# Half-width expert group: tokens as the stationary operand, weights as the moving one, and later weight splits for the next group

## The chip, the cores and the metric

The kernel runs on one core of one Trainium2 chip. The metric is the device time of one execution in microseconds; where several runs were made, their median stands. The profile is one execution of its own, taken by the hardware profiler; a granted TensorE clock of 1.00 means that nothing was throttled.

## What is computed

The reference has two parts. The first is a set of small two-layer networks over x of shape 128 batches x 64 tokens x 256:

```python
s0 = relu(x @ swi[0]) @ swo[0]            # shared, all batches
s1 = relu(x @ swi[1]) @ swo[1]
eo = relu(x @ wi[label]) @ wo[label]      # expert of the batch, 5 experts
w  = softmax(relu(concat(eo[:,0], s0[:,0], s1[:,0]) @ g1) @ g2)
x  = x + eo * w[:,0] + s0 * w[:,1] + s1 * w[:,2]
```

The inner width F is 1024. The second part is one diffusion step with reflected edges on the result, each batch with its own factors. The change concerns only the line `eo`.

## The kernel before

Every fp32 operand of the large products is split into a high part (rounded by a copy on ScalarE) and a low part (the remainder, a subtraction on VectorE or GpSimd), both of type float32r (`split`, L121). A product is then three matmuls: high by high, and the two mixed ones.

A table built on the chip sorts the 128 batches by expert into slots. After the two shared networks' first token tile and five large expert tiles, the remaining slots run as nine groups (`GROUPS`, L31 to L33), in this order: groups 0 to 2 of 8 batches (512 token columns), group 3 of 2 batches (128 columns, "the half", `HALF`), group 4 of 8 batches, groups 5 to 8 of 4 batches (256 columns). Each group is one expert, so it needs its own weights: 4 loads of 512 KB (`load_group_w`, L439), each with two blocks of F of 128, and in each block 256 columns of W-in and 256 of W-out.

A group's work, for each of the eight blocks f of F:

- `split_group_w` (L466) splits the block's 512 weight columns: one copy on ScalarE, one subtraction on VectorE.
- `up` (L918) computes h for this block: six matmuls, with a 128x128 piece of W-in as the stationary operand and the group's token columns as the moving one. h comes out with F on the partitions and tokens in the columns, which is what the next product needs. ScalarE takes the relu as h's high part, VectorE the low part.
- `down` (L932) takes two blocks at a time: 128 tokens of h are the stationary operand, W-out the moving one. Per 128 tokens and block there is a wide matmul (high h by high and low W-out, 512 columns) and a narrow one (low h by high W-out, 256 columns). After the last block `store_group` (L957) adds the two halves of the accumulator (a ScalarE copy, a VectorE addition) and sends them to the table `eo_d` in DRAM.

`stream` (L1011) sets the order. A step is two blocks of F (`LAG`); in each it calls, for both, `ahead` and `up`, and then `down` of the step before. `ahead` (L965) holds everything done in advance: loads of the next or next but one group, the split of its tokens (`split_group_x`, L458; the low part on GpSimd), and one split of the next group's weights per block. Around the half the pattern is bent: during the half only four of group 4's eight splits are made, the other four during group 4's first four blocks, along with those of group 5:

```python
if g == HALF + 1 and f + 4 < NF:
    split_group_w(g, f + 4)
if g + 1 < NRUN:
    if f == (0 if g == HALF else 4):
        split_group_x(g + 1)
    if g != HALF or f < 4:
        split_group_w(g + 1, f)
```

Matmuls and SP's DMA issues are always marked to stay in program order (`mm`, L91; `dma`, L118). VectorE's, ScalarE's and GpSimd's instructions are marked so only while `in_order(True)` holds (L115); in `stream` that is during the half. Elsewhere a scheduler places them. Each of these engines then executes its own queue strictly in the order built, and the same holds for SP, which issues the loads.

Buffers come from pools: 25 tiles of 4 KB per partition for weights, 16 of 2 KB for h and results, and eight PSUM banks, of which six are `psum` and two `seeded`. A tile waits for the last user of the tile that had the buffer before.

Of the kernel before, what the change touches and what calls it, by code (L numbers as in the profile page):

```python
# [8 lines left out]
F32 = mybir.dt.float32  # L9
F32R = mybir.dt.float32r  # L10
I32 = mybir.dt.int32
AF = mybir.ActivationFunctionType
# [4 lines left out]
P = 128  # L17
B, S, D, F = 128, 64, 256, 1024
NE = 5
NF = F // P  # L20
# [8 lines left out]
HALF = NBIG - 1  # L29
# [10 lines left out]
LAG = 2  # L40
# [9 lines left out]
def cond_resid_kernel(ctx: ExitStack, tc: tile.TileContext, xg, xs, xn, itok, z, we, ws, g1, g2, out):  # L50
# [11 lines left out]
    nc = tc.nc  # L62
# [6 lines left out]
    ppool = ctx.enter_context(tc.tile_pool(name="ppool", bufs=6, space=bass.MemoryType.PSUM))  # L69
# [8 lines left out]
    def psum(name):  # L78
        return ppool.tile([P, 512], F32, tag="ps", name=name)
# [5 lines left out]
    def slot4(name, dtype=F32R):  # L85
        return pool4.tile([P, 2, 512], dtype, tag="t4", name=name)

    def slot2(name, dtype=F32):
        return small.tile([P, 512], dtype, tag="s2", name=name)

    def mm(out_ap, lhsT, rhs, start, stop):  # L91
        tc.keep_in_program_order(
            nc.tensor.matmul(out_ap, lhsT=lhsT, rhs=rhs, start=start, stop=stop, skip_group_check=True)  # L93
        )
# [18 lines left out]
    vec, act, gps = (Ordered(engine) for engine in (nc.vector, nc.scalar, nc.gpsimd))  # L113

    def in_order(on):  # L115
        Ordered.on = on

    def dma(dst, src):  # L118
        tc.keep_in_program_order(nc.sync.dma_start(dst, src))

    def split(dst_hi, dst_lo, src, lo_eng):  # L121
        act.activation(dst_hi, src, AF.Copy)
        lo_eng.tensor_tensor(dst_lo, src, dst_hi.bitcast(F32), ALU.subtract)
# [27 lines left out]
    def load_wo(u):  # L151
        wop[u] = slotw(f"wo{u}", [P, 2, 2, D], F32R)
        dma(flat_wo(u), wo_d[u])
# [28 lines left out]
    def load_wi(n, q):  # L182
        u = (n % 2) * NQ + q
        w = win.tile([P, 2, 7, P], F32R, tag="w", name=f"wi{n}_{q}")
        dma(w.bitcast(F32), wi_d[u])
        wip[n * NQ + q] = w
# [4 lines left out]
    def load_x(p, order=((0, 0), (1, 0), (0, 1), (1, 1))):  # L191
        for k, l in order:
            xraw[p, k, l] = slot2(f"xr{p}_{k}{l}")
            dma(xraw[p, k, l], xs[2 * p + l, :, k, :])
# [61 lines left out]
    ident = const.tile([P, P], F32, name="ident")  # L256
# [125 lines left out]
    graw, gw, gxr, gx, gval = {}, {}, {}, {}, {}  # L382
# [3 lines left out]
    def own(g, key, make):  # L386

        if g < NRUN:
            return make()
        if key not in spare:  # L390
            spare[key] = make()
        return spare[key]
# [15 lines left out]
    def load_group_x(g):  # L408
        s0, n = GROUPS[g]
        xr = gxr[g] = group_tile(g, [P, n, 2 * S], F32, "gxr")  # L410
        load_batches(s0, n, lambda j: xr[:, j, :])
# [8 lines left out]
    def group_expert(g):  # L420
        gval[g] = expert_of(GROUPS[g][0])
# [17 lines left out]
    def load_group_w(g):  # L439
        group_expert(g)  # L440
        for h in range(NQ):
            r = own(g, ("raw", h), lambda: slot4(f"gwr{g}_{h}", F32))
            dma(r, we[bass.ds(gval[g], 1), :, 2 * h : 2 * h + 2, :].rearrange("o p f c -> p (o f) c"))
            graw[g, 2 * h], graw[g, 2 * h + 1] = r[:, 0, :], r[:, 1, :]

    def load_group(g):
# [19 lines left out]
    def split_group_w(g, f):  # L466
        w = own(g, ("w", f), lambda: slot4(f"gw{g}_{f}"))
        split(w[:, 0, :], w[:, 1, :], graw[g, f], vec)
        gw[g, f] = w


    eot, yb, sh = {}, {}, {}
# [168 lines left out]
    def run(work):  # L641
        for w in work:
            w()
# [272 lines left out]
    hbuf, gacc, total = {}, {}, []  # L916

    def up(g, f):  # L918
        w, (xh, xl), cols = gw[g, f], gx[g], GROUPS[g][1] * S
        ps = own(g, ("up", f % 2), lambda: (seeded if f % 2 and cols == 512 else psum)(f"up{g}_{f}"))  # L920
        todo = [(k, wp, xx) for k in range(2) for wp, xx in ((0, xh), (0, xl), (1, xh))]
        for i, (k, wp, xx) in enumerate(todo):
            mm(ps[:, :cols], w[:, wp, k * P : (k + 1) * P], xx[:, k, :], i == 0, i == len(todo) - 1)
        hi = own(g, ("h", f), lambda: slot2(f"gh{g}_{f}", F32R))
        lo = slot2(f"gl{g}_{f}", F32R) if cols == 512 else hi[:, 256:512]
        act.activation(hi[:, :cols], ps[:, :cols], AF.Relu)
        vec.scalar_tensor_tensor(
            lo[:, :cols], ps[:, :cols], 0.0, hi[:, :cols].bitcast(F32), ALU.max, ALU.subtract
        )
        hbuf[g, f] = hi, lo  # L930

    def down(g, fs):  # L932

        w = [gw.pop((g, f)) for f in fs]
        m = GROUPS[g][1] * S // P
        h = [hbuf.pop((g, f)) for f in fs]
        if fs[0] == 0:
            gacc[g] = [
                own(g, ("acc", i), lambda: ppool.tile([P, 2, D], F32, tag="ps", name=f"gacc{g}_{i}")) for i in range(m)
            ]  # L940

        def wide(i):
            for j, f in enumerate(fs):
                mm(gacc[g][i], h[j][0][:, i * P : (i + 1) * P], w[j][:, :, 256:512], f == 0, False)

        def narrow(i):
            for j, f in enumerate(fs):
                mm(gacc[g][i][:, 0, :], h[j][1][:, i * P : (i + 1) * P], w[j][:, 0, 256:512], False, f == NF - 1)
            if fs[-1] == NF - 1:
                store_group(g, i)  # L950

        work = [lambda i=i, part=part: part(i) for part in (wide, narrow) for i in range(m)]
        if (g, fs[-1]) == (NRUN - 1, NF - 1):
            return work
        run(work)

    def store_group(g, i):  # L957
        acc = gacc[g][i]
        o = own(g, ("o", i), lambda: small.tile([P, D], F32, tag="s2", name=f"ge{g}_{i}"))
        act.activation(o, acc[:, 0, :], AF.Copy)  # L960
        vec.tensor_add(o, acc[:, 1, :], o)
        r0 = GROUPS[g][0] * S + i * P
        dma(eo_d.rearrange("r (s d) -> (r s) d", d=D)[r0 : r0 + P, :], o)

    def ahead(g, f):  # L965

        if g >= NRUN:
            return
        if f == 0:
            if g == NRUN - 3:  # L970
                slots = nc.values_load(
                    tab[0:1, NSLOT + NU : NSLOT + NU + 1], min_val=0, max_val=NSLOT,
                    skip_runtime_bounds_check_because="the table's entries are bounded on the chip",
                )
                total.append(slots)
            if g + 1 < NRUN:
                if g <= NBIG and g != HALF:
                    load_group_w(g + 1)
                if g != HALF:
                    load_group_x(g + 1)  # L980
            if g < 2:
                reload(g)
            for u in range(3 * g, min(3 * g + 3, 2 * NQ)):
                load_wo(u)
            if g == NRUN - 2:
                load_x(1)
            if g == NRUN - 1:
                load_wi(2, 0)
                load_wi(2, 1)
                load_row()  # L990
        if f == 5 and g < 2:
            again(g)
        if g + 1 == HALF and f == 4:
            load_group_x(g + 2)
        if f == 6 and (g + 1 == HALF or NBIG <= g < NRUN - 2):
            load_group_w(g + 2)
        if g == 0 and f + FIRST < NF:
            split_group_w(0, f + FIRST)
        if g == HALF + 1 and f + 4 < NF:
            split_group_w(g, f + 4)  # L1000
        if g + 1 < NRUN:
            if f == (0 if g == HALF else 4):
                split_group_x(g + 1)
            if g != HALF or f < 4:
                split_group_w(g + 1, f)
        elif f < 7:
            if f < 4:
                sum_x(1, T1 + f, gps)
            split_x(1, (B11, B21, T2, T3, T1, T4, B22)[f], vec)

    def stream(g0, g1):  # L1011
        steps = [(g, tuple(range(f, f + LAG))) for g in range(g0, g1) for f in range(0, NF, LAG)]
        for i in range(len(steps) + 1):
            if i < len(steps):
                in_order(steps[i][0] == HALF)
                for f in steps[i][1]:
                    ahead(steps[i][0], f)
                    up(steps[i][0], f)
            if i >= 1:
                rest = down(*steps[i - 1])  # L1020
        return rest


# [49 lines left out]
    def reload(u):  # L1073
        e, q = divmod(u, NQ)
        load_raw(u, ws[e, :, 2 * q : 2 * q + 2, :])
# [43 lines left out]
    for n in range(EI, EI + NQUAD):  # L1119
        parts = [weights_of(n)]  # L1120
# [14 lines left out]
    rest = stream(0, NRUN)  # L1135
# [61 lines left out]
    for p in range(1, NP):  # L1197
        ta, tb = 2 * p, 2 * p + 1
        for e in range(2):
            n = 2 * p + e  # L1200
            parts = [ahead_w(n)]
# [86 lines left out]
```

## Time and profile before

| | us |
|---|---|
| three runs, median (lowest, highest) | 1038.5 (1038.21, 1038.73) |
| the profiled execution, whole | 1038.9 |
| its span | 1037.1 |
| DMA, mean over the span | 153 GB/s |
| chain that ended last, TensorE's share | 57% |
| groups: first up matmul, last down matmul | 299.1, 444.4 |

The page counts busy time as the time in which an engine has at least one instruction under way. PE is the matmul, PEld the weight load for it, which overlaps matmuls; DVE is VectorE, ACT ScalarE, POOL GpSimd, SP the engine that issues the DMAs. Matmul records overlap each other, so the distance from one start to the next is the cost of one, not the record's length. In the groups of instructions, these rows belong to the nine groups' products:

```profile
L93 PE MATMUL up<-gxh,gw 128*128 128x512 f32 (+2 forms) x288 | 73.4, 329 | 0.0
L93 PE MATMUL gacc<-gw,gh 128*128 128x512 f32 (+1 forms) x272 | 60.8, 363 | 1.7 <-ACT gh L108 1.7
L108 DVE TENSOR_TENSOR gw<-gwr,gw 128x512 fp32r<-128x512 f32 x72 | 54.4, 794 | 9.8 <-ACT gw L108 9.6
```

Columns: line, engine, operation, output and inputs, shape, count, then busy us and mean ns of one, then idle time of the engine just before and what ended most of it. `up` is the first product, `gacc` the second, `gw` a split weight block, `gwr` a loaded one, `gx` tokens, `gh` and `gl` the parts of h, `ge` the stored result.

### The profile page before, as it was taken

How to read it: one execution, taken by the hardware profiler on the slowest of the kernel's cores; microseconds unless marked ns; L12 is line 12 of the kernel's file. 1: busy time of each engine (PE TensorE's matmuls, PEld its weight loads, DVE VectorE, ACT ScalarE, POOL GpSimd, SP SyncE). 2: the span in 40 equal slices, each digit the busy share in tenths (PEclk: the TensorE clock that was granted, in tenths of full speed). 3: DMA queues.
4: the chain of work that ended last, by engine and by line, in shares of the span. 5: the costliest groups of instructions: out<-in, count | busy, mean ns of one | idle time of the engine just before them, and what ended most of it. 6: DMA issues, size and time to landing. Idle time of an engine off the chain costs nothing.

```text
span 1037.1 us, 15675 instructions
## 1 busy us (share of the span) xinstructions
PE 1029.3 (99%) x5423; PEld 881.7 (85%) x5423; DVE 810.9 (78%) x1502; ACT 571.5 (55%) x1080; POOL 155.6 (15%) x165
## 2 busy tenths in 40 slices
PE   9999999999999999999999999999999999999998
PEld 6878888888888879988888888888888888888888
DVE  7998987988777576857989778678687688688776
ACT  6476776776756465643643554455355364355362
POOL 3000000000013000211432220212212212022020
PEclk9999999999999999999999999999999999999999
DMA  6477232331458765555435435334344163253321
GB/s 218 173 270 258 72 116 85 101 122 52 133 189 307 251 206 167 193 205 196 158 127 178 152 108 188 122 122 167 121 159 164 64 219 124 80 192 141 114 77 46
DMA packets 67122, 159.13 MB, mean 153 GB/s; under 512 B 7680, under 2 KB 34688, under 8 KB 67040
## 3 DMA queue, kind: packets, MB, share of 16 engines
q1 hardware_dynamic: 64512, 149.46, 42.2%
q0 software_dynamic: 2384, 8.52, 2.5%
q8 instruction: 43, 0.70, 0.3%
q14 instruction: 39, 0.32, 0.1%
q10 hardware_dynamic: 144, 0.13, 0.0%
HBM read 126.75 MB, written 31.33 MB: 152 GB/s over the span
## 4 chain that ended last, share of the span: by engine, by line
PE 57%; DVE 0%; issue 0%; DVEq 0%
PE acc L93 30%; PE pb L93 11%; PE pd L93 7%; PE pa L93 7%; PE pu L93 1%; PE lin_b L93 0%; PE pgs L93 0%; PE lin_c L93 0%; PE gacc L93 0%; PE pge L93 0%; DVE lq L108 0%; DVE c L108 0%; PE pt_s L510 0%; DVE end_qb L108 0%; PE pl L93 0%
## 5 line engine op out<-in xcount | busy, mean ns | idle before, releaser
L93 PE MATMUL pb<-x,wi 128*128 128x512 f32 x729 | 207.2, 392 | 0.2
L108 ACT ACTIVATE u<-pb 128x512 f32<-128x512 f32 x162 | 97.0, 599 | 114.7 <-PE pb L93 112.6
L93 PEld LDWEIGHTS pb<-x,wi 128*128 128x128 f32 x729 | 130.9, 189 | 23.8 <-ACT u L108 1.2
L93 PE MATMUL pd<-x,wi 128*128 128x512 f32 x486 | 137.9, 392 | 0.3
L93 PE MATMUL pa<-x,wi 128*128 128x512 f32 x486 | 137.1, 390 | 0.3 <-DVEq L1138 0.3
L108 DVE SCALAR_TENSOR_TENSOR yb<-acc,wgt,yb 128x256 f32<-128x256 f32 x216 | 99.3, 482 | 18.1 <-PE acc L93 14.3
L108 ACT ACTIVATE pb<-pa 128x512 f32<-128x512 f32 x81 | 47.2, 582 | 117.7 <-PE pa L93 117.0
L93 PEld LDWEIGHTS pd<-x,wi 128*128 128x128 f32 x486 | 90.8, 188 | 22.2 <-DVE c L108 2.4
L93 PEld LDWEIGHTS pa<-x,wi 128*128 128x128 f32 x486 | 89.8, 188 | 18.5 <-DVEq L1138 0.6
L108 DVE TENSOR_TENSOR c<-pd,u 128x512 f32<-128x512 f32 x81 | 55.9, 690 | 43.2 <-ACT u L108 32.4
L93 PE MATMUL up<-gxh,gw 128*128 128x512 f32 (+2 forms) x288 | 73.4, 329 | 0.0
L108 POOL TENSOR_TENSOR la<-yb 128x508 f32<-128x508 f32 (+1 forms) x28 | 32.2, 1151 | 260.6 <-ACT yb L108 259.0
L93 PE MATMUL gacc<-gw,gh 128*128 128x512 f32 (+1 forms) x272 | 60.8, 363 | 1.7 <-ACT gh L108 1.7
L108 DVE TENSOR_TENSOR gw<-gwr,gw 128x512 fp32r<-128x512 f32 x72 | 54.4, 794 | 9.8 <-ACT gw L108 9.6
L93 PE MATMUL acc<-wo,h_1b 128*128 128x256 f32 (+1 forms) x172 | 56.7, 333 | 0.0
L93 PE MATMUL acc<-wo,h_6b 128*128 128x256 f32 (+1 forms) x172 | 56.7, 334 | 0.0
L93 PE MATMUL acc<-wo,h_7b 128*128 128x256 f32 (+1 forms) x172 | 56.7, 333 | 0.0
L93 PE MATMUL acc<-wo,h_2b 128*128 128x256 f32 (+1 forms) x172 | 56.6, 333 | 0.0
L93 PE MATMUL acc<-wo,h_4b 128*128 128x256 f32 (+1 forms) x172 | 56.5, 332 | 0.0
L93 PE MATMUL acc<-wo,h_3b 128*128 128x256 f32 (+1 forms) x172 | 56.5, 332 | 0.0
L93 PE MATMUL acc<-wo,h_5b 128*128 128x256 f32 (+1 forms) x172 | 56.5, 332 | 0.0
L93 PEld LDWEIGHTS gacc<-gw,gh 128*128 128x128 f32 x272 | 47.4, 188 | 10.7 <-ACT gh L108 2.6
(254 smaller groups left out, 2459.2 us busy)
## 6 DMA issues: line engine op xcount, KB each, us to landing
wi<-wi_d SPq DMA_DIRECT2D x55, 896.0 KB, 4.6
gwr<-we_in SPq DMA_DIRECT2D x32, 512.0 KB, 5.1
wsr<-we_in SPq DMA_DIRECT2D x20, 512.0 KB, 5.3
xr<-xs_in SPq DMA_DIRECT2D x32, 256.0 KB, 5.0
yb<-xn_in SPq DMA_DIRECT2D x16, 512.0 KB, 5.9
y_out<-lq SPq DMA_DIRECT2D x30, 256.0 KB, 2.1
wi_d<-wi SPq DMA_DIRECT2D x8, 896.0 KB, 4.4
xr<-xg_in SPq DMA_DIRECT2D x80, 64.0 KB, 1.9
```

The source lines that it names most:

```text
L93: nc.tensor.matmul(out_ap, lhsT=lhsT, rhs=rhs, start=start, stop=stop, skip_group_check=True)
L108: ins = call(*args, **kwargs)
```

## The change

The half group gets its own path; all other groups keep theirs.

- *Weight splits* (`split_half_w`). The half's weights are split into other tiles: W-in of four blocks of F side by side, high and low in tiles of their own (`hin`), and W-out of two blocks (`hout`). There are still eight splits of 512 columns, one per block, except that two of the old places are empty.
- *Up* (`half_up`). The 128 tokens are the stationary operand, and 512 columns of W-in (four blocks, in four runs of 128) the moving one: 2 x 6 matmuls of 512 columns in place of 48 of 128. h comes out with tokens on the partitions; ScalarE takes the relu in fp32, two of 512 columns.
- *Turn* (`half_turn`). Eight fp32 transposes of 128x128 on TensorE bring h back, four to a PSUM bank; each bank is then split, a copy on ScalarE and a subtraction on VectorE.
- *Down* (`half_down`). The same 8 wide and 8 narrow matmuls, all wide ones first.
- *Order* (`stream`). The half is one step in place of four. TensorE's order is: half up; down of group 2's last two blocks; the transposes; up of group 4's first two blocks; half down; up of group 4's next two.
- *Group 4's first step* is in program order too, and group 5's weight splits start later: none in group 4's first two blocks, then one each, two, two, one and one.

```diff
--- before.py
+++ after.py
@@ -441,6 +441,7 @@
         for h in range(NQ):
             r = own(g, ("raw", h), lambda: slot4(f"gwr{g}_{h}", F32))
             dma(r, we[bass.ds(gval[g], 1), :, 2 * h : 2 * h + 2, :].rearrange("o p f c -> p (o f) c"))
+            graw[g, "both", h] = r
             graw[g, 2 * h], graw[g, 2 * h + 1] = r[:, 0, :], r[:, 1, :]
 
     def load_group(g):
@@ -467,6 +468,58 @@
         w = own(g, ("w", f), lambda: slot4(f"gw{g}_{f}"))
         split(w[:, 0, :], w[:, 1, :], graw[g, f], vec)
         gw[g, f] = w
+
+
+    hin, hout, hid = {}, {}, {}
+
+    def split_half_w(f):
+
+        h = f // 2
+        r = graw[HALF, "both", h]
+        if f % 2:
+            w = hout[h] = slot4(f"ho{h}").rearrange("p h c -> p (h c)").rearrange("p (f h c) -> p f h c", f=2, h=2)
+            split(w[:, :, 0, :], w[:, :, 1, :], r[:, :, 256:512], vec)
+        else:
+            if h % 2 == 0:
+                for part in range(2):
+                    t = slot4(f"hi{h // 2}{part}")
+                    hin[h // 2, part] = t.rearrange("p h c -> p (h c)").rearrange("p (f c) -> p f c", f=4)
+            hi, lo = (hin[h // 2, part][:, h % 2 * 2 : h % 2 * 2 + 2, :] for part in range(2))
+            split(hi, lo, r[:, :, 0:256], vec)
+
+    def half_up():
+        parts = gx[HALF]
+        for j in range(2):
+            ps = psum(f"hu{j}")
+            todo = [(k, wp, xp) for k in range(2) for wp, xp in ((0, 0), (1, 0), (0, 1))]
+            for i, (k, wp, xp) in enumerate(todo):
+                w = hin[j, wp][:, :, k * P : (k + 1) * P]
+                mm(ps, parts[xp][:, k, :], w, i == 0, i == len(todo) - 1)
+            hid[j] = slot2(f"hr{j}")
+            act.activation(hid[j], ps, AF.Relu)
+
+    def half_turn():
+        for j in range(2):
+            pt = psum(f"ht{j}")
+            for i in range(4):
+                cols = slice(i * P, (i + 1) * P)
+                tc.keep_in_program_order(nc.tensor.transpose(pt[:, cols], hid[j][:, cols], ident))
+            hi, lo = slot2(f"hth{j}", F32R), slot2(f"htl{j}", F32R)
+            split(hi, lo, pt, vec)
+            hid[j] = hi, lo
+
+    def half_down():
+        acc = gacc[HALF] = [ppool.tile([P, 2, D], F32, tag="ps", name="hacc")]
+        for wide in (True, False):
+            for f in range(NF):
+                j, i = divmod(f, 4)
+                w = hout[f // 2][:, f % 2, :, :]
+                cols = slice(i * P, (i + 1) * P)
+                if wide:
+                    mm(acc[0], hid[j][0][:, cols], w, f == 0, False)
+                else:
+                    mm(acc[0][:, 0, :], hid[j][1][:, cols], w[:, 0, :], False, f == NF - 1)
+        store_group(HALF, 0)
 
 
     eot, yb, sh = {}, {}, {}
@@ -1001,7 +1054,12 @@
         if g + 1 < NRUN:
             if f == (0 if g == HALF else 4):
                 split_group_x(g + 1)
-            if g != HALF or f < 4:
+            if g + 1 == HALF:
+                split_half_w(f)
+            elif g == HALF + 1:
+                for k in ((), (), (0,), (1,), (2, 3), (4, 5), (6,), (7,))[f]:
+                    split_group_w(g + 1, k)
+            elif g != HALF or f < 4:
                 split_group_w(g + 1, f)
         elif f < 7:
             if f < 4:
@@ -1009,15 +1067,31 @@
             split_x(1, (B11, B21, T2, T3, T1, T4, B22)[f], vec)
 
     def stream(g0, g1):
-        steps = [(g, tuple(range(f, f + LAG))) for g in range(g0, g1) for f in range(0, NF, LAG)]
+        steps = []
+        for g in range(g0, g1):
+            n = NF if g == HALF else LAG
+            steps += [(g, tuple(range(f, f + n))) for f in range(0, NF, n)]
         for i in range(len(steps) + 1):
             if i < len(steps):
-                in_order(steps[i][0] == HALF)
-                for f in steps[i][1]:
-                    ahead(steps[i][0], f)
-                    up(steps[i][0], f)
+                g, fs = steps[i]
+                in_order(g == HALF or (g == HALF + 1 and fs[0] == 0))
+                if g == HALF:
+                    for f in fs[:2]:
+                        ahead(g, f)
+                    half_up()
+                    for f in fs[2:]:
+                        ahead(g, f)
+                else:
+                    for f in fs:
+                        ahead(g, f)
+                        up(g, f)
             if i >= 1:
-                rest = down(*steps[i - 1])
+                if steps[i - 1][0] == HALF:
+                    half_down()
+                else:
+                    rest = down(*steps[i - 1])
+            if i < len(steps) and g == HALF:
+                half_turn()
         return rest
```

On SP's queue as built, two of group 5's four weight loads now stand ahead of the four stores of group 2's results, which they followed before; group 6's four loads all follow the store of the half's result.

## The prediction

> **What bounds the kernel.** First the page: its busy times and the span in slices.
>
> ```profile
> span 1037.1 us, 15675 instructions
> PE 1029.3 (99%) x5423; PEld 881.7 (85%) x5423; DVE 810.9 (78%) x1502; ACT 571.5 (55%) x1080; POOL 155.6 (15%) x165
> PEclk9999999999999999999999999999999999999999
> ```
>
> TensorE has work in 99% of the span at full granted clock. Busy matmul records overlap and do not prove a peak, but they show where TensorE stands still: 1037.1 - 1029.3 = 7.8 us in all. Next, the busy time of each engine by stage (columns: stretch, its length, then busy us of PE, PEld, DVE, ACT, POOL, the clock, DMA share, GB/s).
>
> ```profile
> 299.00:361.00 62.00, 62.00 (x313) 52.83 (x312) 42.77 (x68) 35.91 (x71) 11.29 (x11) 1.00 0.81 278
> 361.00:380.00 19.00, 17.26 (x110) 14.98 (x110) 12.09 (x25) 10.34 (x27) 2.40 (x1) 1.00 0.54 186
> 380.00:436.00 56.00, 56.00 (x366) 51.12 (x365) 42.36 (x81) 36.16 (x85) 10.82 (x8) 1.00 0.63 202
> ```
>
> The groups run from 299 to 445 us, and the half-width group lies in the middle row, the only one of the three with idle TensorE: 1.74 us. Before it and after it TensorE never waits, and from 450 to 1025 us the same view gives it 574.9 of 575. So a microsecond that TensorE saves at 362 to 379 us should move the end by one. Third, TensorE's own order of time there (start, length, what; in brackets the idle time before it and its releaser).
>
> ```profile
> 362.45 0.22 PE L93 MATMUL up<-gxh,gw 128*128 128x128 f32 x1
> ...
> 363.75 2.07 PE L93 MATMUL gacc<-gw,gh 128*128 128x512 f32 x8
> 365.65 1.11 PE L93 MATMUL gacc<-gw,gl 128*128 128x256 f32 x8
> 366.60 0.22 PE L93 MATMUL up<-gxh,gw 128*128 128x128 f32 x1
> ...
> 376.65 0.49 PE L93 MATMUL gacc<-gw,gh 128*128 128x512 f32 x1 [1.03 <-ACT gh L108]
> 377.86 0.82 PE L93 MATMUL gacc<-gw,gh 128*128 128x512 f32 x3 [0.71 <-ACT gh L108]
> 378.52 0.40 PE L93 MATMUL up<-gxh,gw 128*128 128x512 f32 x1
> ```
>
> I take 362.45 (the half's first matmul) to 378.52 (the third F block of group 4) as the stretch that changes: 16.07 us. Its two stalls are explained by ScalarE's order of time.
>
> ```profile
> 370.31 0.62 ACT L108 ACTIVATE gw<-gwr 128x512 fp32r<-128x512 f32 x1
> 375.29 1.15 ACT L108 ACTIVATE gw<-gwr 128x512 fp32r<-128x512 f32 x2 [4.36 <-DMA gwr<-we_in]
> 376.35 0.26 ACT L108 ACTIVATE gh<-up 128x128 fp32r<-128x128 f32 x1
> ```
>
> The half's relu at 376.35 stands in ScalarE's queue behind a weight split of group 5, whose load landed only at 375.3. The split itself was in no hurry; the relu was.
>
> **The old stretch, summed.** Four blocks of 12 up-matmuls of 128 columns: 362.45 to 363.75, 366.60 to 367.89, 368.64 to 369.93, 370.69 to 371.98: 5.17 us, 0.108 each. Group 2's last down step: 2.85. The half's down steps, four pairs at about 0.76: 3.0. Group 4's first two F blocks, 12 matmuls of 512 columns at 0.227 to 0.229: 2.75. The stalls, taken from start to start: 376.65 less the 375.47 at which the matmul before was through (1.18), and 377.86 less 376.88 (0.98): 2.16. Sum 15.9 of 16.07.
>
> **The change, part by part.** *Up.* 48 matmuls of 128 columns become 12 of 512. At the row of group 4's up step this is 12 x 0.229 = 2.75, so -2.4. Both stream 6144 columns, and here a rule speaks against the change: the Trainium skill, TensorE: Matmul & The Clock Gate, section Back-to-back issue gap, gives an isolated matmul N/2.4 ns plus 2.5. By it 48 x 55.8 = 2.68 against 12 x 215.8 = 2.59, and nothing is gained. The row decides: 0.108 each, with a weight load every 0.11 us beside it, so at 128 columns the load sets the pace. The new moving operand has four runs of 128 elements at a stride. No row shows that; the nearest, the down step's W-out operand in two runs of 256, streams at 0.226. I take 0.229; from above, if each run cost what a matmul of 128 columns does, 4 x 0.108 = 0.43 each, 5.2, and the gain is gone; below the column rate it cannot be.
>
> *Transposes.* Eight of 128x128 in fp32 are added. The gate has four such:
>
> ```profile
> 444.53 0.60 PE L510 MATMUL pt_s<-ident,row 128*128 128x128 f32 x4
> 444.89 0.94 PE L93 MATMUL pb<-x,wi 128*128 128x512 f32 x3
> ```
>
> Four in 0.36, or 0.44 in the chain of waits: eight cost 0.7 to 0.9; I take 0.9. The same page, section Part 4: PE-mode transpose, states about 275 ns for one inside a kernel, which would be 2.2 and take 1.3 off the gain. The row is of the same shape, type and clock and wins; 2.2 is the upper bound.
>
> *Down.* Same 8 wide and 8 narrow matmuls, now in one piece: 8 x 0.227 + 8 x 0.118 = 2.75, so -0.25.
>
> *ScalarE and VectorE.* The half's weight splits keep their number and elements, in other slices: nothing. Eight small relus (0.28) and eight small subtractions (0.28) become two relus (0.60), two copies (0.62) and two subtractions (0.68) of 512: about 0.1 and 0.9 less. Their cover is what matters, since the half's chain now goes TensorE, ScalarE, TensorE, ScalarE and VectorE, TensorE. I lay the built order of the changed kernel on these durations, from 362.45:
> - Up ends at 365.2. Group 2's last down step covers the relus (2.85, to 368.05). ScalarE holds two group-4 splits, the relus, two more splits, four store copies, the two transposed copies. The second relu is done at 366.0: 2.0 us spare. Behind the transposes' new wait stands all of group 4.
> - Transposes to 368.95. Then group 4's first up matmul needs the PSUM bank of group 2's first accumulator. VectorE has four group-4 splits ahead of that addition; the first was 2.47 us long in the old trace (beside GpSimd's 2.40), the others 0.68. It frees the bank at about 368.3: 0.6 spare, the thinnest cover.
> - Group 4's up runs to 371.7 and covers the transposed copies, done at 370.0, and subtractions, done at 370.7 and needed only by the narrow matmuls at 373.5.
> - The half's down ends at 374.5. ScalarE's copy of its result waits for that; a group-5 split and group 4's third relu stand behind it, needed only from 380 us on.
>
> *The later splits.* Group 5's split no longer stands before any of the half's work: the 2.16 goes. Next is TensorE itself; I find no wait in its place.
>
> *DMA.* Same transfers. On SP's queue two of group 5's four loads move ahead of group 2's four stores (the old trace issued the stores from 366.95 and the loads from 371.0); they can start at about 360, when their slots come free, in a stretch with DMA share 0.11. The other two stay behind the stores, which wait for VectorE's additions, and land near 376, ten microseconds before they hold anything up. Group 6's first two loads stay near 376; the others come forward from 383.4. Cost nothing.
>
> **Sum.** 2.75 + 2.85 + 0.9 + 2.75 + 2.75 = 12.0 against 16.07: 4.0 us less. The profiled execution took 1038.9 (span 1037.1 and 1.8 around it), so it would take 1034.9; the median of the runs shown is 0.4 below it: 1034.5.
>
> **Rivals.**
> 1. *The wait comes back in another place*: a landing like the old 4.36 falls ahead of the transposed copies on ScalarE. Spare there is 1.9, so 2.4 is lost, gain 1.6: 1036.9. For it: ScalarE's queue is in order, and full. Against: the loads of group 4 that stand there were issued from 354.6 and DMA was nearly idle from 361 to 366.
> 2. *The strided moving operand does not stream*: up stays at 5.2, gain 1.6: 1036.9. Against: the W-out row.
> 3. *The gain is given back*: groups 5 to 8 catch up with their loads: 1038.5. Against: TensorE never waited from 380 to 436 at DMA share 0.63.
> 4. *Slower, by VectorE*: its splits and additions from here on all run at the 2.47-for-0.68 of the split beside GpSimd. Then three splits cost 5.4 more, the first addition 1.1, and the bank comes at 374.8 instead of 368.3: TensorE is 5.9 late. Three more additions at 1.5 and two transposed subtractions at 2.47 end at 384.2, 4.8 after the narrow matmuls are due. Late by 10.7 against 4.0 gained: about 1045. It decides from 4.6 us of lag at the first addition. Against: GpSimd has one instruction in this window, counted already.
>
> **Chances.** My sum 0.77 (1033.9 to 1035.3); something between 2.1 and 3.2 gained (transposes at the page's price) 0.08; rival 1 0.05, 2 0.03, 3 0.03, 4 0.04. So faster by over 0.2% (2.1 us, about what a measurement of this kernel can tell) 0.85, within 0.11, slower 0.04. The range reaches from a gain of 4.7 (transposes at 0.7, seams gone) to 1.9.
>
> **What would show it.** Right: 12 up matmuls about 0.23 apart; eight transposes within 0.9; no idle TensorE with ScalarE as releaser; the third block of group 4 at about 374.5; groups 5 to 8 unchanged in length. Wrong: a gap ahead of the transposes or of group 4's first up (VectorE's addition), up matmuls 0.4 apart, transposes near 0.28, or new waits after 380.

## The result, and the profile after

| | before | after |
|---|---|---|
| median of 7 runs, us | 1038.5 (1037.86 to 1039.0) | 1034.74 (1033.99 to 1036.53) |
| the profiled execution, whole, and its span, us | 1038.9, 1037.1 | 1034.74, 1032.7 |

After to before is 0.9964, 95% interval 0.9955 to 0.9973: 3.8 us less (2.8 to 4.7), where 4.0 were forecast. The page of the changed kernel:

```profile
span 1032.7 us, 15598 instructions
PE 1027.2 (99%) x5395; PEld 880.3 (85%) x5395; DVE 811.0 (79%) x1496; ACT 572.8 (55%) x1076; POOL 155.6 (15%) x165
```

Span less TensorE's busy time is now 5.5 us in place of 7.8. The busy time of each engine by stage, with stretches that answer to those of before:

```profile
299.00:361.00 62.00, 62.00 (x313) 52.82 (x312) 43.26 (x68) 35.80 (x71) 11.28 (x11) 1.00 0.81 274
361.00:376.00 15.00, 15.00 (x83) 13.02 (x82) 10.85 (x18) 9.73 (x20) 2.41 (x1) 1.00 0.59 197
376.00:432.00 56.00, 56.00 (x366) 51.24 (x365) 43.29 (x82) 38.12 (x87) 11.31 (x8) 1.00 0.64 215
```

The middle row has lost its idle TensorE, and the groups after it still run without any. TensorE in order of time:

```profile
362.52 0.63 PE L93 MATMUL hu<-hi,gxh 128*128 128x512 f32 x2
...
365.27 1.98 PE L93 MATMUL gacc<-gw,gh 128*128 128x512 f32 x8
367.08 1.11 PE L93 MATMUL gacc<-gw,gl 128*128 128x256 f32 x8
368.03 1.04 PE L506 MATMUL ht<-ident,hr 128*128 128x128 f32 x8
368.82 0.47 PE L93 MATMUL up<-gxh,gw 128*128 128x512 f32 x1
...
371.65 1.98 PE L93 MATMUL hacc<-ho,hth 128*128 128x512 f32 x8
373.47 1.11 PE L93 MATMUL hacc<-ho,htl 128*128 128x256 f32 x8
374.42 0.40 PE L93 MATMUL up<-gxh,gw 128*128 128x512 f32 x1
```

From the half's first matmul (362.52) to group 4's third block (374.42) it is 11.90 us; before it was 16.07. Below, "the stretch" is this distance. It is the best measure of a variant, since whole times scatter: the kernel before gave medians from 1038.5 to 1038.83 in the batches below, with single runs from 1036.26 to 1042.55. But it comes from one profiled execution of each kernel. ScalarE after:

```profile
365.47 0.60 ACT L108 ACTIVATE hr<-hu 128x512 f32<-128x512 f32 x1 [0.76 <-PE hu L93]
365.96 1.14 ACT L108 ACTIVATE gw<-gwr 128x512 fp32r<-128x512 f32 x2
367.51 1.21 ACT L108 ACTIVATE ge<-gacc 128x256 f32<-128x256 f32 x4 [0.41 <-PE gacc L93]
368.67 1.09 ACT L108 ACTIVATE hth<-ht 128x512 fp32r<-128x512 f32 x2
```

No wait for a load (`gwr`) is left here. ScalarE waits for TensorE, and not the other way round. The gain is also kept to the end of the groups: from the half's first matmul to the first transpose of the gate (`pt_s`) it was 82.08 us (362.45 to 444.53), and is now 77.87 (362.52 to 440.39).

### The profile page after: what moved, and what is told of

Same layout as the page of the kernel before. It is cut to its first block, busy times and chain, and to the rows that moved or that the text cites. A ratio compares the mean times of both kernels' runs of the same rounds, so it can differ in the third digit from the quotient of the medians.

```text
span 1032.7 us, 15598 instructions
## 1 busy us (share of the span) xinstructions
PE 1027.2 (99%) x5395; PEld 880.3 (85%) x5395; DVE 811.0 (79%) x1496; ACT 572.8 (55%) x1076; POOL 155.6 (15%) x165
## 4 chain that ended last, share of the span: by engine, by line
PE 57%; DVE 0%; issue 0%; DVEq 0%
PE acc L93 30%; PE pb L93 11%; PE pd L93 7%; PE pa L93 7%; PE pu L93 1%; PE lin_b L93 0%; PE pgs L93 0%; PE lin_c L93 0%; PE gacc L93 0%; PE pge L93 0%; DVE lq L108 0%; DVE c L108 0%; PE pt_s L563 0%; DVE end_qb L108 0%; PE pl L93 0%
## 5 line engine op out<-in xcount | busy, mean ns | idle before, releaser
L93 PE MATMUL up<-gxh,gw 128*128 128x512 f32 (+1 forms) x256 | 67.7, 337 | 0.0
L93 PE MATMUL gacc<-gw,gh 128*128 128x512 f32 (+1 forms) x256 | 56.6, 363 | 0.0
L93 PE MATMUL acc<-wo,h_0b 128*128 128x256 f32 (+1 forms) x172 | 56.4, 332 | 0.0
L108 DVE TENSOR_TENSOR pd<-pd,u 128x512 f32<-128x512 f32 x81 | 55.8, 689 | 0.7 <-PE pd L93 0.6
```

What stands on the lines that cost most here:

```text
L108: ins = call(*args, **kwargs)
```

## The experiments

Theory 2 is the prediction's: the old stall of 2.2 us goes because group 5's splits come later. Theory 1, formed from the built order, is its rival: it goes because the new path lets two of group 5's loads be issued some 11 us earlier. The stretches first (us from the profiled execution), with the whole times beside them. In the code cuts `...` marks lines that are left out.

| run | stretch | median, us | to the kernel before (95%) |
|---|---|---|---|
| before | 16.07 | 1038.5 | 1 |
| changed kernel again | 11.90 | 1034.39 | 0.9956 (0.9941 to 0.9972) |
| new path, old splits | 11.90 | 1034.88 | 0.9960 (0.9945 to 0.9974) |
| old path, later splits | 13.70 | 1037.2 | 0.9986 (0.9978 to 0.9993) |
| the same, first step unordered | 14.13 | 1037.93 | 0.9992 (0.9983 to 1.0001) |
| old path, loads early | 14.83 | 1037.83 | 0.9988 (0.9977 to 0.9999) |
| the later splits, half the columns | 13.66 | 1036.7 | 0.9974 (0.9963 to 0.9985) |
| transposes twice | 12.77 | 1035.6 | 0.9961 (0.9949 to 0.9973) |
| transposes four times | 14.52 | 1038.06 | 0.9995 (0.9986 to 1.0004) |
| VectorE lag, one | 12.00 | 1034.78 | 0.9959 (0.9945 to 0.9972) |
| VectorE lag, four | 15.78 | 1037.84 | 0.9986 (0.9978 to 0.9993) |
| VectorE lag of eight, later | 14.49 | 1038.26 | 0.9987 (0.9975 to 0.9999) |
| GpSimd beside | 16.59 | 1039.24 | 0.9999 (0.9990 to 1.0008) |

**The changed kernel again**, no edit.

> The changed kernel once more, for comparison on the same chip. Both theories: 3.7 to 4.2 us under the kernel before, no stall of TensorE in the half.

It came out so: the stretch is 11.90, without a stall.

**The new path alone.**

```diff
-            elif g == HALF + 1:
-                for k in ((), (), (0,), (1,), (2, 3), (4, 5), (6,), (7,))[f]:
-                    split_group_w(g + 1, k)
...
-                in_order(g == HALF or (g == HALF + 1 and fs[0] == 0))
+                in_order(g == HALF)
```

> The half's new path alone: group 5's weight splits start again with group 4's first block, and program order holds during the half only. In the queue as built a split of group 5 stands ahead of group 4's first relus. Theory 1 (the loads' place did it): group 5's first load is issued near 360 us because the one-step half puts it ahead of the stores, so the split finds its data and nothing waits; all of the gain stays, 4.1 us. Theory 2 (the later splits did it, as the prediction put it): the split holds ScalarE again and about 2.2 us are lost; gain 1.9.

It came out as theory 1 forecast: the stretch is the changed kernel's to the hundredth, and the whole times do not differ beyond their scatter. ScalarE of this run, where splits of groups 4 and 5 stand among each other:

```profile
369.66 2.19 ACT L108 ACTIVATE gw<-gwr 128x512 fp32r<-128x512 f32 x4
371.75 0.60 ACT L108 ACTIVATE gh<-up 128x512 fp32r<-128x512 f32 x1
```

Four splits run without a pause from 369.66, two of them group 5's, where before one waited 4.36 us for its data. Group 5's first two loads are part of an unbroken series of six issues from 354.40 to 360.66; before, they were issued from 371.00. SP, in this run and then before:

```profile
354.40 6.26 SPq L119 DMA_DIRECT2D gwr<-we_in  x6
371.00 2.09 SPq L119 DMA_DIRECT2D gwr<-we_in  x4
```

The new path brings a second thing along: the last of ScalarE's work that the half's matmuls need, the two transposed copies from 368.69, stands ahead of these splits in ScalarE's queue. By this order a late load would have held group 4's relus, which TensorE needs from 377.19, but not the half's matmuls. No run has the new path with late loads, so the two are not told apart here.

**The later splits alone.**

```diff
+            if g == HALF + 1:
+                for k in ((), (), (0,), (1,), (2, 3), (4, 5), (6,), (7,))[f]:
+                    split_group_w(g + 1, k)
-            if g != HALF or f < 4:
+            elif g != HALF or f < 4:
                 split_group_w(g + 1, f)
...
-                in_order(steps[i][0] == HALF)
+                in_order(steps[i][0] == HALF or steps[i] == (HALF + 1, (0, 1)))
```

> The later splits alone: the half keeps its 48 up matmuls and four steps; group 5's splits start in group 4's third block and group 4's first step is in program order. Theory 2: the two stalls of 2.2 us go, nothing else changes; gain 2.1, and the stretch from the half's first matmul to group 4's third block is 13.9 us. Theory 1: the load still lands at 375 behind the stores, and the wait moves to another instruction in ScalarE's queue; gain under 1.

It came out as theory 2 forecast: the stretch is 2.37 shorter, although the loads still stand behind the stores (issued from 369.71). The half's last down step, which held the stalls of 1.03 and 0.71, has none:

```profile
374.70 0.85 PE L93 MATMUL gacc<-gw,gh 128*128 128x512 f32 x4
```

So either part of the change, the new path or the later splits, removes the whole stall. The median gained 1.4 us, with an interval from 0.7 to 2.3. The way from 13.70 here to the changed kernel's 11.90, 1.80, is what the new path itself is worth.

**The same without program order in group 4's first step.**

> As the run with the later splits alone, but without program order in group 4's first step. As built, group 5's first split then stands between the relus of the half's seventh and eighth blocks. Theory 2 in the form that the place in the queue matters: the eighth relu waits for the landing at 375.3, one stall of about 1.2 to 1.5 us stays; gain 0.6 to 1.0. If only the number of splits matters: gain 2.1 as with order.

```profile
371.43 0.27 ACT L108 ACTIVATE gh<-up 128x128 fp32r<-128x128 f32 x1
374.15 1.16 ACT L108 ACTIVATE gw<-gwr 128x512 fp32r<-128x512 f32 x2 [2.46 <-DMA gwr<-we_in]
375.21 0.26 ACT L108 ACTIVATE gh<-up 128x128 fp32r<-128x128 f32 x1
```

The split stands ahead of the eighth relu as built, and the wait is there, 2.46 us. But the data landed a microsecond earlier than in the old trace, the relu came at 375.21, and only some 0.4 us of it reached TensorE: 14.13 against 13.70. The place in the queue matters, as expected; the size, 1.2 to 1.5, was too large. In whole time this run cannot be told from the kernel before.

**The old path with early loads.** In `ahead`:

```diff
-                if g <= NBIG and g != HALF:
+                if g <= NBIG and g != HALF and g != HALF + 1:
                     load_group_w(g + 1)
...
+        if g == HALF and f == 1:
+            load_group_w(g + 2)
```

> The kernel before, with group 5's four weight loads put ahead of group 2's four stores on SP's queue (issued during the half's first step); the half keeps its 48 up matmuls, and the splits of group 5 still start with group 4's first block. As built, several of them stand ahead of the half's relus on ScalarE. Theory 1 (the late landing made the stall): the splits find their data, the stretch from the half's first matmul to group 4's third block is about 13.9 in place of 16.07, gain about 2.1. Theory 2 (a split in that place of the queue makes the stall): 16 or more, no gain.

The result lies in between: 14.83. TensorE's two stalls of 1.03 and 0.71 shrink to one of 0.45 and some smaller ones, and no split waits for its load any more. What is left, 1.1 us against the later splits alone, comes from ScalarE being full: three splits at a time stand between the half's relus.

```profile
369.25 1.70 ACT L108 ACTIVATE gw<-gwr 128x512 fp32r<-128x512 f32 x3
370.82 0.31 ACT L108 ACTIVATE gh<-up 128x128 fp32r<-128x128 f32 x1
370.97 1.71 ACT L108 ACTIVATE gw<-gwr 128x512 fp32r<-128x512 f32 x3
372.54 0.31 ACT L108 ACTIVATE gh<-up 128x128 fp32r<-128x128 f32 x1
```

So both theories hold in part for the old path: early loads alone take back 1.24 of the 2.37 that the later splits take, and the rest is the splits' place in the queue. On the new path the place did not matter in the run with the old splits; there the half's matmuls need only two relus and two copies of ScalarE, all ahead of group 5's first split.

**Half the columns**, on the run with the later splits alone:

```diff
+            n = 64 if g == HALF and i > 0 else cols
-            mm(ps[:, :cols], w[:, wp, k * P : (k + 1) * P], xx[:, k, :], i == 0, i == len(todo) - 1)
+            mm(ps[:, :n], w[:, wp, k * P : (k + 1) * P], xx[:, k, :n], i == 0, i == len(todo) - 1)
```

> The run with the later splits alone, with 40 of the half's 48 up matmuls over 64 token columns in place of 128 (the others' contribution for the second batch is left out). If the weight load sets the pace at 0.108: no change to that run, matmuls still 0.108 apart. If columns do: 40 x 27 ns = 1.1 us less.

The stretch is 13.66 against 13.70. The first two blocks' 12 matmuls run from 361.67 to 362.93, 0.105 each, against 361.69 to 362.98, 0.108. So the columns do not set the pace. What is left is the pair of weight load and matmul: before, the weight loads fill the block from 362.5 to 363.7 without a gap (1.20 us of 1.20), while at 512 columns they fill 1.66 of 2.00 (373 to 375). That it is the load, and not some other fixed cost of the pair, is the likely reading; no run here has one without the other.

**Transposes twice.**

```diff
-            for i in range(4):
-                cols = slice(i * P, (i + 1) * P)
+            for i in range(8):
+                cols = slice(i % 4 * P, (i % 4 + 1) * P)
```

> The changed kernel with every transpose made twice, 16 for 8, the second overwriting the first. By the gate's row (0.09 to 0.11 each): 0.8 us slower than the changed kernel, 3.2 under the one before. By the 275 ns of the skill's page: 2.2 slower, 1.9 under the one before.

Sixteen run from 367.49 to 369.16, 1.67 in all or 0.104 each. The stretch is 0.87 longer. The gate's row was right as the cost of one; the 275 ns were not.

**VectorE lag**: four, then one, unread subtractions between the step's splits and the addition that frees the PSUM bank.

```diff
+            if i < len(steps) and g == HALF:
...
+                for _ in range(4):
+                    vec.tensor_tensor(lagged, graw[g + 1, 3], graw[g + 1, 3], ALU.subtract)
```

> The changed kernel with four further VectorE subtractions of 128x512 that nobody reads (0.61 apart), ahead of the addition that frees group 4's PSUM bank: 2.45 us of lag. If the cover there is 0.5 to 0.6 as worked out, TensorE stands still 1.9 us ahead of group 4's first up matmul, 1.9 slower than the changed kernel. If the cover is larger (the first up matmul waits for something else), less; over 2.4 cannot be.

> The changed kernel with one further VectorE subtraction that nobody reads ahead of the addition that frees group 4's PSUM bank: 0.61 of lag. If the cover is 0.5 to 0.6: TensorE waits 0.0 to 0.2 us there, and the stretch from the half's first matmul to group 4's third block is 11.9 to 12.1.

One costs 0.1 in the stretch: the cover (the time by which the bank is free before TensorE needs it) is there, and about as thin as worked out. Four give the expected standstill:

```profile
371.13 0.50 PE L93 MATMUL up<-gxh,gw 128*128 128x512 f32 x1 [2.01 <-DVE ge L108]
...
371.70 1.02 PE L93 MATMUL up<-gxh,gw 128*128 128x512 f32 x2
```

But the stretch grows by 3.9, not by 1.9, since the 12 matmuls behind the standstill take 4.45 us in place of 2.83. The stages show why (the third column from the right is the granted clock):

```profile
371.00:372.00 1.00, 0.86 (x3) 0.78 (x4) 1.00 (x5) 0.00 (x0) 0.00 (x0) 0.86 0.04 13
372.00:373.00 1.00, 1.00 (x4) 0.71 (x4) 1.00 (x3) 0.00 (x0) 0.00 (x0) 0.50 0.89 274
...
375.00:376.00 1.00, 1.00 (x5) 0.79 (x4) 0.53 (x1) 0.22 (x1) 0.00 (x0) 0.93 0.56 157
```

The clock was halved from about 371.7 to 375.1, and full before and after. Two runs tell whether the standstill did that or the transposes ahead of it.

**A standstill away from the transposes**: eight subtractions like those above, in `half_turn`, ahead of the transposed subtractions.

> The changed kernel with eight further VectorE subtractions that nobody reads, behind the addition that frees the PSUM bank and ahead of the transposed subtractions: 4.9 us of lag against the 2.9 of cover worked out there, so TensorE stands still about 2.0 us between the half's wide and narrow matmuls, away from the transposes. The run with four subtractions showed a granted clock of 0.50 for some 3.4 us after a standstill of 2.0 us that followed eight transposes. If the standstill alone lowers the clock: 0.50 here too, 3.6 us in all slower than the changed kernel. If the transposes before it count as standstill: clock 1.00, 2.0 slower.

**Transposes four times**: `range(16)` in place of `range(8)` in the edit above.

> The changed kernel with every transpose made four times, 32 for 8: TensorE transposes for 3.4 us without a pause. At 0.105 each 2.5 us slower than the changed kernel if the clock stays at 1.00. If transposes count as standstill for the clock, as the skill's page on TensorE says, the granted clock falls to 0.50 behind them or within them, and it is about 4 us slower.

One row of each run, the first with its standstill above it:

```profile
375.17 1.53 PE L93 MATMUL hacc<-ho,htl 128*128 128x256 f32 x8 [2.06 <-DVE htl L108]
377.00:378.00 1.00, 1.00 (x4) 0.81 (x3) 1.00 (x2) 0.64 (x2) 0.00 (x0) 0.50 0.08 22
370.00:371.00 1.00, 1.00 (x11) 1.00 (x10) 0.69 (x1) 0.17 (x1) 0.00 (x0) 1.00 0.59 190
```

The standstill does it without the transposes. In the first of these runs TensorE stands still for 2.06 between the half's wide and narrow matmuls, and the clock falls to 0.50 from about 376.1 to 379.5 us; by then the stretch is nearly over, which is why it is only 14.49. In the second, 32 transposes from 367.63 to 371.04 (0.107 each) leave the clock at 1.00 in every stage from 365 to 377, and none of its 20 executions had a mean clock under 0.999. So the statement that its expectation takes from the Trainium skill (TensorE: Matmul & The Clock Gate, Part 4: PE-mode transpose), that a transpose does not count as busy for the clock, is not what this run shows. The stretch of this run is as expected (2.6 longer). Its median is 3.3 above the run with a lag of one on the same chip, where the stretches differ by 2.5; single runs reach from 1036.35 to 1040.88, and that scatter stays unexplained.

**GpSimd beside**: at the place of the VectorE lag, on a tile of 128x1024:

```diff
+                for _ in range(3):
+                    gps.tensor_tensor(lagged, graw[g + 1, "both", 1], graw[g + 1, "both", 1], ALU.subtract)
```

> The changed kernel with three further GpSimd subtractions of 128x1024 that nobody reads (2.4 us each) right after the one of group 4's tokens, so that they run beside VectorE's splits and additions until about 371 us. If GpSimd stretches VectorE as beside the first split (2.47 for 0.68): two splits end near 371, the bank comes near 371.6, TensorE is 2.7 us late; 1.3 under the kernel before. If it was a single accident: splits at 0.68, no change to the changed kernel's time.

GpSimd is busy to 370.5, and VectorE beside it:

```profile
361.69 9.38 DVE L108 TENSOR_TENSOR gw<-gwr,gw 128x512 fp32r<-128x512 f32 x4 [0.78 <-ACT gw L108]
```

Four splits take 9.38, against 3.08 and 1.29 for the same four in the changed kernel. The stretching is no accident. TensorE stood still for 2.81, 3.05 later than in the changed kernel (2.7 expected), and then ran at half clock too, from about 371.5 to 374.9. Of the 1.3 us of gain that were expected to be left, none was.

## Why the prediction was right, and where it was not

*Up*: 2.75 predicted, 362.52 to 365.27 measured: 2.75. The four strided runs of the moving operand stream like a contiguous one; rival 2 did not occur. The rule of N/2.4 ns would have seen no gain, and the run with half the columns shows that at 128 columns it does not hold for this stream. The section that the prediction cites says so itself: it gives the rule for an isolated matmul, and says that it is too low at small N because it has no weight load in it.

*Transposes*: 0.9 predicted, 0.79 measured. The page's 275 ns fits the length of one record, 272 ns here; the prediction tried it as the distance from one start to the next, and that is 99 ns.

*Down*: 2.75 predicted, 2.77 measured. *Group 2's down*: 2.85 taken over, 2.76 measured. *Group 4's up*: 2.75 taken over, 2.83, the first matmul behind the transposes being some 0.1 longer.

*The sum*: 12.0 predicted, 11.90 measured, so 4.17 gained in the stretch. The two spans differ by another 0.2 (4.4 in all); no edit explains that, and it is within what single runs scatter by. The median gave 3.8. In the sum the new path and the end of the stall stand apart as 1.8 and 2.2; the run with the later splits alone measures them as 1.80 and 2.37, so more than half of the gain is the stall.

*ScalarE's work* was added up wrongly: eight relus of 0.28 become two of 0.60 and two copies of 0.62, which is 0.2 more and not 0.1 less. Nothing hung on it, since TensorE does not wait for ScalarE in the stretch.

*The covers*: second relu done at 366.0 predicted, 366.07 measured; the bank free at 368.3 predicted, 368.35 measured. The thinnest cover was named rightly: 0.6 against some 0.5 in the trace (free at 368.35, needed at 368.82), which the lag runs bear out.

*The later splits: right in amount, incomplete as a cause.* The prediction said that the 2.16 goes because group 5's split no longer stands before the half's work, and booked the loads' new place on SP's queue as "Cost nothing". The later splits do remove the stall where they stand alone (13.70). But the new path with the old splits has the same stretch as the changed kernel, 11.90: beside the new path the later splits bring nothing that these runs can see. The prediction did not look at what the new path alone does to the stall. How the new path does it is not settled: its loads come earlier, which alone takes back 1.24 on the old path, and none of its half's matmuls needs anything of ScalarE that stands behind group 5's splits. That the amount came out right was partly luck, because either part of the change would have been enough for the stall.

*The price of a late VectorE* was mis-sized: rival 4 and the lag were reckoned at one microsecond per microsecond. After a standstill of 2.0 the clock takes up to 1.6 more. So where the clock falls, the lag that uses up the gain is about 3.0 us and not 4.6 (an estimate: 4.6 less 1.6). Rival 4's cause is real, and 7 us of further GpSimd work are enough to lose all the gain. It did not occur because GpSimd has 2.4 us to do there.

Rivals 1 and 3 did not occur: no load is waited for in the stretch, and from 376 to 432 TensorE is never idle.

## What to carry to other kernels

Where a matmul's moving side is as narrow as 128 columns, look at the distance between starts and not at columns. Here it did not shrink with the columns, and swapping the operands paid 1.80 us of 13.70, even with the transposes that it asks for; every hand-over to another engine had a matmul block beside it. When an edit removes a stall, ask which of its parts would have removed it alone; here two would, and only running each alone showed that. Lay the built queues on measured durations instruction by instruction: in this case that gave every hand-over inside the half to within 0.3 us.

## What the hardware showed beyond that

A standstill of TensorE of 2.0 us was enough to halve the granted clock for 3.4 us, beginning 0 to 1.0 us after work resumed in the three profiled executions (371.7 after 371.13, 376.1 after 375.17, and, after the 2.8 us beside GpSimd, at once at 371.5). By the mean clock this happened in some executions and not in others. With the lag of four, 7 of 15 executions had a mean clock of 0.998 in place of 0.999 or more, and their median was 1038.53 against 1037.16; with the lag of eight, 7 of 12, 1038.69 against 1037.22; with the 2.8 us beside GpSimd, 11 of 14, 1039.4 against 1037.79. So 1.4 to 1.6 us each time, on top of the standstill. The Trainium skill (TensorE: Matmul & The Clock Gate, Part 1) describes a free-running window of about 3.4 us, which fits the length and the chance in it. The same page's table in Why this matters for your kernels warns only of gaps above about 3 us, which was too generous here. The kernel before, with its two short stalls, had 0.998 or less in 12 of 118 executions of these batches, the changed kernel, the new path alone, the transposes twice and the lag of one in none of 33. On one of the four chips the kernel before had none in 35 executions either, and that the old stall caused those 12 was not traced.

The fp32 transposes kept a full clock up: 3.4 us of nothing else, at 1.00. A subtraction of VectorE with two SBUF inputs ran 2.3 to 2.5 us in place of 0.6 to 0.7 for as long as a subtraction of GpSimd was under way.
